# Three attentions of a four-block kernel: row maxima sent by DMA into the queries' tiles, remainders formed in pairs, the work of a round dealt anew

## The chip, the cores and the metric

The kernel runs on one core of a Trainium2 chip. The metric is the device time of one execution in microseconds; the time before is the median of three runs. Beside them stands one execution that was taken with the hardware profiler. All durations below come from that execution.

## The reference, cut to what matters

Four blocks follow each other on x of shape (4, 512, 288): an attention with a mixture of four experts, an attention with a dense layer, a rotation in a subspace, and another attention with a dense layer. All in float32. The change touches the three attentions (called 0, 1 and 3 after their blocks), each of 16 heads of 18 features:

```python
q, k, v = (h @ w_qkv + b_qkv) split into 16 heads of 18
attn = softmax(q @ k^T * 18 ** -0.5)          # per batch and head, 512 x 512
o = attn @ v
x = x + gate * (o @ w_proj + b_proj)
```

## The kernel before, in words

**Rounds and gaps.** An attention works off 16 rounds `r`, one for each batch `b` (4) and group `g` of four heads (4). A round has eight gaps `k` (`gaps = 2 * NT`). Each gap begins with a *quad* (`quad`): two row-max products (`row_max`, tiles a0m, a1m, a3m) for the present round, and two products for the weights (`weight`, tiles a0s, a1s, a3s) that lag ten gaps behind, so they belong to the round before or the one before that. The four products of a quad use 32 rows each (a head has 18 features, padded to 32), lie on the four row groups of TensorE, and run there together. Each fills one PSUM bank of 128x512. VectorE empties the banks of the row maxima (`tensor_reduce`, L1115), ScalarE those of the weights (`Exp`, L1127).

**What fills a gap after its quad.** `shift(r - 1)` in gap 0: the maxima stand in a tile `maxima` with one column for each head and query tile; four transposes on TensorE (tile a3sh and its like) bring them into rows, and VectorE subtracts them (L1170) from row 18 of each head's padded queries. The padded keys hold a one there, so the product for the weights already has the maximum taken off. `sums`: the weights of one key tile times the values (tile av, with a column of ones for the denominators); two key tiles in gap 2 and two in gap 6. `steps[k]`: layer norm, division, biases and loads. `pieces[k]`: a string of letters, each of which moves a job on by one step: Q (`queries_and_keys`, tiles psqk), X (`values`, tiles psv), P (`project`, tiles pp), A (`activations`, transposes), R (the experts' routing, in attention 0).

**Jobs.** A features' length of 288 is two chunks of 128 and a remainder of 32 (36 rows for `project`). A job's product is thus one remainder product and two whole chunks (four half-width ones for queries and keys). The remainder of tile or chunk `n` stands on row group `n % 4`; for `project` on one half of the array. Before, jobs take one tile after the other.

**Queries and keys on their way.** `queries_and_keys` leaves chunks of seven heads in an SBUF tile; DMAs from POOL's queue (L1055) spread each head's 18 rows to 32-row places in `pads`, which has `NR = 3` places for queries and three for keys. Before a place is used again POOL clears it (L193), and rows that came too early wait in `waiting`.

**Banks.** PSUM has eight banks of this size: four of tag "sc", three of tag "de", one for av. In the main loop of an attention (`wide`) each call of `bank` takes its tag from a ring:

```python
banks = {"sc": 4, "de": 3}
ring, turns, wide = ["sc"] * 4 + ["de"] * 2, [0], [False]
...
        if wide[0]:
            turns[0] += 1
            tag = ring[turns[0] % len(ring)]
```

Quads call `bank`, and so does `misc` (the transposes of `shift` and of `activations`, the routing). Jobs call `place`, which in the main loop takes a "de" bank by name, without the ring. A tile takes any free bank of its tag, and keeps it until it has been evicted.

**Order.** TensorE's products run in the order of the program (`mm` orders each behind the last). After the 16 rounds a last loop of five steps does the weights that lag, and then the hidden layer that follows begins. Attention 0 has other work beside it: `tick` moves a chain of reflections on VectorE and POOL (the subspace of the rotation), four times in a round, then twice; in attention 1 twice.

Of the kernel before, what the change touches and what calls it, by code (L numbers as in the profile page):

```python
# [25 lines left out]
NR = 3  # L26
# [22 lines left out]
def kernel(ctx: ExitStack, tc: tile.TileContext, a: dict, out: bass.AP):  # L49
# [128 lines left out]
    maxima = []  # L178
    for n in range(2):
        m = cst.tile([P, NT, NG * DP], F32, tag=f"max{n}", name=f"max{n}")  # L180
        nc.gpsimd.memset(m, 0.0)
        maxima.append(m)
    zeros = maxima[0].rearrange("p t c -> p (t c)")
# [4 lines left out]
    nc.vector.tensor_reduce(unit, ident[:, D::DP], AX.X, ALU.add)  # L188

    def cleared(engine, k):  # L190

        if k < NR:
            engine.memset(pads[:, k, :], 0.0)  # L193
        else:
            engine.tensor_copy(pads[:, k, :], unit.to_broadcast([P, T]))
# [95 lines left out]
    def attention_weights(l):  # L291
# [71 lines left out]
        def clear(engine, *some):  # L363
            return both(*[lambda k=k: cleared(engine, k) for k in some])

# [3 lines left out]
        order = (0, NR, 1, NR + 1, 2, NR + 2)  # L369
        if l == 0:  # L370
            late.append(clear(nc.gpsimd, *order))
        else:
            late += [clear(nc.vector, *order[0:3]), clear(nc.vector, *order[3:])]
# [171 lines left out]
    def warm(name, n):  # L545

        ps = bank("sc", name)
        for _ in range(n):
            mm(ps[:, 0 : T // 2], lhsT=ident, rhs=zeros[:, 0 : T // 2], start=True, stop=True)
            ordered(last[0], turned_rows[0])  # L550
# [450 lines left out]
    def attention(l, w, mod, eps, feed, ticks, hT=None, then=None, also=()):  # L1001
# [11 lines left out]
        with ExitStack() as es:  # L1013
            pool = es.enter_context(tc.tile_pool(name=name, bufs=2))
            hTs, xns, vs, raws, outs, gbs = {}, {}, {}, {}, {}, {}
            dens, ps, now = {}, {}, [0, True]
            waiting = []
# [5 lines left out]
            def place(what):  # L1023
                return misc(what) if now[1] else single("de", what)

            def values(b, *tiles):

                for t in tiles:
                    yield
                    if t == 0:  # L1030
                        vs[b] = pool.tile([P, NT, H, D + 1], F32, tag="v", name=f"{name}v{b}")
                        nc.gpsimd.memset(vs[b][:, :, :, D : D + 1], 1.0)
                    ps = place(f"{name}psv{b}_{t}")
                    for c in (MC, *range(MC)):
                        if c < MC:
                            yield
                        mm(
                            ps[:, 0:C],
                            lhsT=rows_of(hTs[b], c, t, slice(t * P, (t + 1) * P)),
                            rhs=rows_of(w["v"], c, t, slice(0, C)),  # L1040
                            start=(c == MC),
                            stop=(c == MC - 1),
                        )
                    o = vs[b][:, t, :, 0:D]
                    i = ps[:, 0:C].rearrange("p (h d) -> p h d", d=D)
                    if "bv" in w:
                        bv = w["bv"].rearrange("p (h d) -> p h d", d=D)
                        nc.vector.tensor_add(o, i, bv)
                    else:
                        nc.vector.tensor_copy(o, i)  # L1050

            def send(r, s, i, row, queue):

                to = pads[i * DP : i * DP + D, s * NR + r % NR, :]
                queue.dma_start(to, row)  # L1055

            def sent(r):

                for one in [one for one in waiting if one[0] == r]:
                    waiting.remove(one)  # L1060
                    send(*one, nc.gpsimd)

            def queries_and_keys(*some):

                for b, n in some:
                    yield
                    ps = place(f"{name}psqk{b}_{n}")
                    m = min(HC, 2 * H - n * HC) * D
                    rows, first = rest_of(n)
                    mm(  # L1070
                        ps[0:m, :],
                        lhsT=w["qkr"][rows, first : first + m],
                        rhs=hTs[b][rows, MC, :],
                        start=True,
                        stop=False,
                    )
                    for q in (slice(0, T // 2), slice(T // 2, T)):
                        for c in range(MC):
                            yield
                            mm(  # L1080
                                ps[0:m, q],
                                lhsT=w["qk"][:, c, n * HC * D : n * HC * D + m],
                                rhs=hTs[b][:, c, q],
                                start=False,
                                stop=(c == MC - 1 and q.stop == T),
                            )
                    t = pool.tile([HC * D, T], F32, tag="qk", name=f"{name}qk{b}_{n}", bufs=3)
                    nc.scalar.activation(  # L1088
                        t[0:m], ps[0:m], AF.Identity, bias=w["bqk"][0:m, n : n + 1]
                    )  # L1090
                    for g, s, i, k, at in heads_of(n):
                        for j in range(k):
                            row = t[(at + j) * D : (at + j + 1) * D, :]
                            one = (b * NG + g, s, i + j, row)
                            if one[0] < NR or one[0] <= now[0] + 1:
                                queue = nc.scalar if s and one[0] == 0 and n == 0 and i + j else nc.gpsimd
                                send(*one, queue)
                            else:
                                waiting.append(one)

            def heads_rows(i):
                return slice(i * DP, (i + 1) * DP)

            def row_max(r, t, i):

                m = maxima[r % 2].rearrange("p t (h d) -> p t h d", d=DP)
# [3 lines left out]
                    lhsT=pads[heads_rows(i), r % NR, t * P : (t + 1) * P],  # L1110
                    rhs=pads[heads_rows(i), NR + r % NR, :],
# [3 lines left out]
                take("DVE", nc.vector.tensor_reduce(m[:, t, i, D : D + 1], ps, AX.X, ALU.max))  # L1115

            def weight(r, t, i):
                ps = bank("sc", f"{name}s{r}_{t}_{i}")
                mm(
                    ps,  # L1120
                    lhsT=pads[heads_rows(i), NR + r % NR, t * P : (t + 1) * P],
                    rhs=pads[heads_rows(i), r % NR, :],
# [33 lines left out]
            def shift(r):  # L1156

                ps = misc(f"{name}sh{r}")
                m = maxima[r % 2]
                for t in range(NT):  # L1160
                    mm(
                        ps[:, t * P : (t + 1) * P],
                        lhsT=m[:, t, :],
                        rhs=ident,
                        is_transpose=True,
                        start=True,
                        stop=True,
                    )
                q = pads[:, r % NR, :]
                take("DVE", nc.vector.tensor_sub(q, q, ps))  # L1170
# [71 lines left out]
            def project(b, *groups):  # L1242
# [3 lines left out]
                for tiles in groups:  # L1246
                    yield
                    o = outs[b, "o"]
                    ps = [place(f"{name}pp{b}_{t}") for t in tiles]
# [29 lines left out]
            def others(r):  # L1279
# [7 lines left out]
                pieces = {1: "QQ", 3: "QQQ", 4: "PPP", 5: "PP", 7: "P"}  # L1287
                if b < 2:
                    pieces = {0: "Q", 1: "Q", 3: "Q", 4: "QQ"}
# [9 lines left out]
                if g < NG - 1 and b < B:  # L1299
                    jobs["Q"] = queries_and_keys((b, g + 2))  # L1300
                elif b + 1 < B:
                    jobs["Q"] = queries_and_keys((b + 1, 0), (b + 1, 1))
# [7 lines left out]
                if g == 1 and b + 1 < B:  # L1310
                    jobs["A"] = activations(b + 1)
                    jobs["X"] = values(b + 1, 0)
                    pieces = {0: "AA", 1: "QQ", 2: "A", 3: "QQQ", 4: "XXX", 5: "PP", 7: "P"}
                    if b < 2:
                        pieces.update({4: "X", 5: "X", 7: "X"})
                if g == 2 and b + 1 < B:
                    jobs["X"] = values(b + 1, 1, 2, 3)
                    pieces = {0: "XXX", 1: "QQ", 3: "QQQ", 4: "XXX", 5: "X", 7: "XX"}
                if g == 3 and b + 1 < B:
                    pieces = {0: "QQ", 1: "QQQ", 3: "QQ", 4: "QQQ", 5: "PP", 7: "P"}  # L1320
                    if b == 0:
                        pieces = {0: "QQ", 1: "QQQ", 3: "QQ", 4: "QQ", 5: "Q"}
                if r == n - 4:
                    pieces = {0: "PPP", 1: "QQ", 3: "QQQ", 4: "PPP", 5: "PP", 7: "P"}
                if r == n - 3:
                    pieces = {0: "Q", 1: "Q", 3: "Q", 4: "QQ"}
                if r == n - 2:
                    pieces = {0: "Q", 1: "Q", 3: "Q", 4: "QQ"}
                if r == n - 1:
                    pieces = {1: "PPP", 3: "PP", 4: "P", 5: "PP", 7: "P"}  # L1330


                if g == 2 and 0 < b < B:
                    for c in range(MC + 1):
                        steps[c].append(lambda c=c: divide(b - 1, c))
                if 0 <= r - 2 < n:
# [1346 lines left out]
```

## Time and profile before

| | us |
|---|---|
| median of 3 runs (lowest, highest) | 1905.28 (1903.22, 1907.09) |
| the profiled execution | 1910.58 |
| its span, first to last instruction | 1908.6 |
| TensorE busy in the span | 1852.5 (97%) |
| VectorE busy | 1069.1 (56%) |
| POOL busy | 743.9 (39%) |
| ScalarE busy | 720.8 (38%) |
| first to last quad, attentions 0, 1, 3 | 29 to 405, 862 to 1201, 1408 to 1742 |

Starts and durations are of the profiled execution, in us from its first instruction. TensorE's matmuls are pipelined and the ends of its rows are modelled; the time from the start of one item to the start of the next is what the item costs in the queue. One product in float32 gives two rows in the trace (two matmul instructions). PE is TensorE, PEld its weight loads, DVE VectorE, ACT ScalarE, POOL GpSimd, SP the engine whose queue starts most DMAs. In a row of the timeline stand the start, the length, the engine, the line, the operation, the written and read tiles, the shapes and the number of instructions that were merged; in brackets the idle time before it and what ended it.

### The profile page before, as it was taken

How to read it: one execution, taken by the hardware profiler on the slowest of the kernel's cores; microseconds unless marked ns; L12 is line 12 of the kernel's file. 1: busy time of each engine (PE TensorE's matmuls, PEld its weight loads, DVE VectorE, ACT ScalarE, POOL GpSimd, SP SyncE). 2: the span in 40 equal slices, each digit the busy share in tenths (PEclk: the TensorE clock that was granted, in tenths of full speed). 3: DMA queues.
4: the chain of work that ended last, by engine and by line, in shares of the span. 5: the costliest groups of instructions: out<-in, count | busy, mean ns of one | idle time of the engine just before them, and what ended most of it. 6: DMA issues, size and time to landing. Idle time of an engine off the chain costs nothing. (4 is left out here: it accounts for less than half of the span.)

```text
span 1908.6 us, 28581 instructions
## 1 busy us (share of the span) xinstructions
PE 1852.5 (97%) x10037; PEld 954.6 (50%) x10037; DVE 1069.1 (56%) x3171; ACT 720.8 (38%) x1347; POOL 743.9 (39%) x1204
## 2 busy tenths in 40 slices
PE   7999999998989998999999999999999999999998
PEld 4333333356767776774333333555643334334565
DVE  4767877725534555548767668252265666573201
ACT  1545545343222222223545455422125555455121
POOL 6253543434334346535734353222523344442101
PEclk9989999899989999999999999999999999999999
DMA  6442222326676666641312111300101221111000
GB/s 158 121 59 49 33 70 69 94 57 191 181 196 201 184 185 190 204 130 42 75 40 45 43 42 37 75 15 4 24 17 28 45 57 40 40 42 23 19 17 25
DMA packets 100547, 151.14 MB, mean 79 GB/s; under 512 B 42432, under 2 KB 77803, under 8 KB 100405
## 3 DMA queue, kind: packets, MB, share of 16 engines
q0 software_dynamic: 35280, 87.64, 16.5%
q1 hardware_dynamic: 64850, 61.45, 13.9%
q8 instruction: 80, 1.31, 0.3%
q14 instruction: 63, 0.51, 0.1%
q10 hardware_dynamic: 274, 0.23, 0.0%
HBM read 103.24 MB, written 20.08 MB: 65 GB/s over the span
## 5 line engine op out<-in xcount | busy, mean ns | idle before, releaser
L1115 DVE TENSOR_REDUCE max<-a3m 128x1 f32<-128x512 f32 x256 | 164.3, 684 | 103.6 <-PE a3s L89 100.0
L1115 DVE TENSOR_REDUCE max<-a1m 128x1 f32<-128x512 f32 x256 | 164.9, 683 | 72.0 <-PE a1s L89 68.8
L1115 DVE TENSOR_REDUCE max<-a0m 128x1 f32<-128x512 f32 x256 | 164.7, 682 | 62.1 <-PE a0s L89 59.4
L1127 ACT ACTIVATE a0p<-a0s 128x512 f32<-128x512 f32 x256 | 140.4, 596 | 155.3 <-PE a0s L89 143.7
L1127 ACT ACTIVATE a1p<-a1s 128x512 f32<-128x512 f32 x256 | 139.3, 596 | 138.0 <-PE a1s L89 132.9
L1127 ACT ACTIVATE a3p<-a3s 128x512 f32<-128x512 f32 x256 | 139.0, 596 | 133.1 <-PE a3s L89 129.7
L89 PE MATMUL e0h<-e0hT,e0w 128*128 128x256 f32 (+1 forms) x918 | 172.6, 400 | 5.4 <-ACT e0hT L2239 2.8
L89 PE MATMUL e0o<-e0w,e0hm 128*128 128x288 f32 x648 | 171.7, 415 | 3.1 <-DVE ef L966 3.1
L89 PE MATMUL a0m<-pads 32*128 32x512 f32 x512 | 165.6, 660 | 6.9 <-DVE max L1115 6.2
L89 PE MATMUL a0s<-pads 32*128 32x512 f32 x512 | 169.0, 673 | 1.6 <-ACT a0p L1127 1.4
L89 PE MATMUL a1s<-pads 32*128 32x512 f32 x512 | 159.8, 642 | 3.2 <-DVE max L1115 3.2
L89 PE MATMUL a1m<-pads 32*128 32x512 f32 x512 | 157.7, 640 | 0.3 <-DVE max L1115 0.2
L89 PE MATMUL a3s<-pads 32*128 32x512 f32 x512 | 156.4, 637 | 0.0
L89 PE MATMUL a3m<-pads 32*128 32x512 f32 x512 | 153.4, 636 | 1.1 <-DVE max L1115 1.1
L89 PEld LDWEIGHTS e0h<-e0hT,e0w 128*128 128x128 f32 (+1 forms) x918 | 131.3, 193 | 40.5 <-issue 17.4
L89 PEld LDWEIGHTS e0o<-e0w,e0hm 128*128 128x128 f32 x648 | 121.9, 193 | 36.0 <-DVE ef L966 3.9
L1588 ACT ACTIVATE e0hm<-e0h,e0w 128x256 f32<-128x256 f32 x144 | 60.3, 470 | 126.4 <-PE e0h L89 102.5
L2150 POOL DMA_INDIRECT e0w<-w1c,wrow x57 | 55.4, 971 | 123.3 <-PE e0h L89 66.7
L89 PEld LDWEIGHTS a0m<-pads 32*128 32x128 f32 x512 | 49.7, 189 | 69.5 <-DVE max L1115 33.2
L1055 POOL DMA_DIRECT2D pads<-a3qk x126 | 63.4, 509 | 52.8 <-ACT a3qk L1088 21.8
L89 PE MATMUL f1h<-f1hT,w 128*128 128x512 f32 (+1 forms) x216 | 81.2, 616 | 0.8 <-ACT f1hT L620 0.4
L1055 POOL DMA_DIRECT2D pads<-a0qk x126 | 64.0, 513 | 45.2 <-ACT a0qk L1088 14.8
(546 smaller groups left out, 3286.0 us busy)
## 6 DMA issues: line engine op xcount, KB each, us to landing
eo<-e0r SPq DMA_DIRECT2D x50, 144.0 KB
ada<-in_ada SPq DMA_DIRECT2D x18, 324.0 KB
wr<-in_wrot SPq DMA_DIRECT2D x16, 288.0 KB
xm<-e0m SPq DMA_DIRECT2D x6, 768.0 KB
pads<-a0qk POOLq DMA_DIRECT2D x126, 36.0 KB
pads<-a1qk POOLq DMA_DIRECT2D x126, 36.0 KB
pads<-a3qk POOLq DMA_DIRECT2D x126, 36.0 KB
g<-gates SPq DMA_DIRECT2D x24, 144.0 KB
```

The costliest lines, as they stand in the source:

```text
L89: ins = nc.tensor.matmul(*args, **kwargs).ins
L1055: queue.dma_start(to, row)
L1115: take("DVE", nc.vector.tensor_reduce(m[:, t, i, D : D + 1], ps, AX.X, ALU.max))
L1127: take("ACT", nc.scalar.activation(p, ps, AF.Exp, scale=D**-0.5))
L1588: nc.scalar.activation(self.hms[i][f], ps[r], func, bias=b1(f)),
L2150: gather = nc.gpsimd.indirect_dma_start(dst, None, table, bass.IndirectOffsetOnAxis(row, 0))
```

## The change

*Maxima.* They are written to a 128x32 tile, a column for each head and query tile. `shift(r)` comes at the end of round `r` (gap 7): VectorE transposes the tile in blocks of 32x32, and four DMAs from POOL's queue send the rows into row 18 of the padded queries. The padded keys hold minus one there, written once (`marked`). TensorE's transposes and VectorE's subtraction go. Row-max products use 18 rows of each head, products for the weights 19.

*Places and lag.* `NR` is 4, the clearing by POOL and the list `waiting` go, the weights lag twelve gaps (`LAG`), and the last loop has six steps. `sums` takes one key tile in each of gaps 0, 2, 4 and 6.

*Pairs.* `values`, `queries_and_keys` and `project` take two tiles or chunks at a time (some chunks of queries and keys stay single): first both remainders, then the chunks of the one and of the other. The first has a "de" bank, the second an "sc" bank.

*The deal.* `pieces` and `steps` are set anew; the experts' own setting for the last round goes.

```diff
-NR = 3
+NR = 4
+LAG = 12
...
+        m = cst.tile([P, DP], F32, tag=f"max{n}", name=f"max{n}")
...
+        rows_of_maxima.append(cst.tile([P, DP], F32, tag=f"mrow{n}", name=f"mrow{n}"))
...
+    nc.vector.tensor_scalar_mul(unit, unit, -1.0)
+    def marked(engine, k):
+        engine.tensor_copy(pads[:, NR + k, :], unit.to_broadcast([P, T]))
+    overwritten = 2 * (MC + 1) - NR
+    for k in range(overwritten, NR):
+        marked(nc.vector, k)
...
+            def place(what, k=0):
+                return misc(what) if now[0] else single(("de", "sc")[k], what)
...
+                    ps = [place(f"{name}psv{b}_{t}", k) for k, t in enumerate(tiles)]
...
+                    for k in range(len(tiles)):
+                        product(k, MC)
+                    for k, t in enumerate(tiles):
                         for c in range(MC):
                             yield
+                            product(k, c)
...
+            def queries_and_keys(b, *groups):
+                for ns in groups:
+                    yield
+                    ps = [place(f"{name}psqk{b}_{n}", k) for k, n in enumerate(ns)]
...
             def row_max(r, t, i):
+                rows = slice(i * DP, i * DP + D)
...
+                k = i * NT + t
+                to = maxima[r % 2][:, k : k + 1]
+                take("DVE", nc.vector.tensor_reduce(to, ps, AX.X, ALU.max))
             def weight(r, t, i):
+                rows = slice(i * DP, i * DP + D + 1)
...
             def shift(r):
-                for t in range(NT):
-                    mm(
-                        ps[:, t * P : (t + 1) * P],
-                        lhsT=m[:, t, :],
-                        rhs=ident,
-                        is_transpose=True,
...
-                q = pads[:, r % NR, :]
-                take("DVE", nc.vector.tensor_sub(q, q, ps))
+                m, t = maxima[r % 2], rows_of_maxima[r % 2]
+                take("DVE", nc.vector.transpose(t, m))
+                to = pads[D::DP, r % NR, :].rearrange("i (t k j) -> i t k j", k=P // DP, j=DP)
+                for k in range(P // DP):
+                    nc.gpsimd.dma_start(to[:, :, k, :], t[k * DP : k * DP + GH * NT, :])
...
-                pieces = {1: "QQ", 3: "QQQ", 4: "PPP", 5: "PP", 7: "P"}
+                pieces = {1: "QQ", 3: "QQQ", 5: "PP", 7: "PPP"}
                 if b < 2:
-                    pieces = {0: "Q", 1: "Q", 3: "Q", 4: "QQ"}
+                    pieces = {1: "QQ", 3: "QQ", 4: "Q"}
...
+                some = {0: [2], 1: [3, 4], 3: [0, 1]}
+                if b == B - 1:
+                    some = {0: [2], 1: [3], 2: [4]}
+                own = b + (g == NG - 1)
+                if own < B and g in some:
+                    jobs["Q"] = queries_and_keys(own, some[g])
...
                 if g == 1 and b + 1 < B:
                     jobs["A"] = activations(b + 1)
+                    pieces = {1: "QQ", 2: "A", 3: "QQQ", 4: "A", 5: "QQ", 6: "A", 7: "QQ"}
                 if g == 2 and b + 1 < B:
+                    jobs["X"] = values(b + 1, [0, 1], [2, 3])
+                    pieces = {1: "XXX", 3: "XX", 5: "XXX", 7: "XX"}
+                if g in (1, 2) and b == B - 1:
+                    pieces = {1: "QQ", 3: "QQ", 4: "Q"}
                 if g == 3 and b + 1 < B:
+                    pieces = {0: "QQ", 1: "QQQ", 2: "Q", 3: "QQQ", 5: "PP", 7: "PPP"}
+                if g == 3 and b == B - 1:
+                    pieces = {1: "P", 3: "PP", 5: "P", 7: "P"}
                 if g == 2 and 0 < b < B:
                     for c in range(MC + 1):
-                        steps[c].append(lambda c=c: divide(b - 1, c))
-                if 0 <= r - 2 < n:
-                    steps[5].append(lambda: invert(r - 2))
+                        steps[c + 2].append(lambda c=c: divide(b - 1, c))
+                if 0 <= r - 2 < n - 2:
+                    steps[7].append(lambda: invert(r - 2))
                 if g == 0 and b > 1:
+                    jobs["P"] = project(b - 2, [1, 3])
                 if g == 3 and b > 0:
+                    jobs["P"] = project(b - 1, [0, 2])
...
-                    quad([(row_max, r, k)] + lagging(8 * r + k - 10))
-                    if k == 0:
-                        shift(r - 1)
+                    quad([(row_max, r, k)] + lagging(gaps * r + k - LAG))
+                    if k == gaps - 1:
+                        shift(r)
                     for step in steps[k]:
                         step()
-                    if k == 2 and r > 1:
-                        sums(r - 2, 2)
-                        sums(r - 2, 3)
                     if k == 6:
                         sums(r - 1, 0)
-                        sums(r - 1, 1)
+                    elif k % 2 == 0 and r > 1:
+                        sums(r - 2, 1 + k // 2)
                     work_off(jobs, pieces.get(k, ""))
...
+            for k in range(LAG // 2):
+                u = gaps * n + 2 * k - LAG
+                quad(lagging(u) + lagging(u + 1))
```

## The prediction

> **What bounds the kernel now.** I read the page first: TensorE is busy for 1852.5 of 1908.6 us, VectorE for 56%. A busy TensorE can still be a waiting one, so I then asked for the busy time by stage, over the three attentions.
>
> ```profile
> 1408.00:1742.00 334.00, 331.27 (x1970) 128.21 (x1968) 214.89 (x412) 168.24 (x300) 128.61 (x235) 0.99 0.18 39
> 862.00:1201.00 339.00, 334.51 (x1969) 128.82 (x1962) 254.23 (x601) 168.85 (x300) 157.62 (x268) 0.99 0.20 46
> 29.00:405.00 376.00, 363.09 (x2108) 145.06 (x2106) 276.92 (x747) 171.31 (x307) 156.51 (x269) 0.95 0.33 75
> ```
>
> Columns: window, its length, busy time of PE, PEld, DVE, ACT, POOL, then granted clock and DMA. In all three TensorE (third column) fills the window; VectorE stands at 64 to 75%. So a round lasts as long as TensorE's queue of it, plus what that queue waits. The timeline of attention 3 shows the queue item by item; start to start is the price.
>
> ```profile
> 1550.08 0.69 PE L89 MATMUL a3m<-pads 32*128 32x512 f32 x1
> ...
> 1551.15 1.91 PE L89 MATMUL av<-a3p,a3v 128*19 128x512 f32 x16
> 1551.24 1.29 DVE L1115 TENSOR_REDUCE max<-a3m 128x1 f32<-128x512 f32 x2 [1.27 <-PE a3s L89]
> 1551.28 1.09 ACT L1127 ACTIVATE a3p<-a3s 128x512 f32<-128x512 f32 x2 [0.41 <-PE a3s L89]
> ...
> 1552.99 0.69 PE L89 MATMUL a3m<-pads 32*128 32x512 f32 x1
> ...
> 1553.98 1.02 PE L89 MATMUL a3psqk<-a3hT,wqkr 32*126 32x512 f32 x2
> ...
> 1554.92 0.70 PE L89 MATMUL a3psqk<-a3hT,wqk 128*126 128x256 f32 x2
> ...
> 1559.18 1.43 PE L89 MATMUL a3pp<-wp,a3oo 36*128 36x288 f32 x4
> ...
> 1560.55 0.69 PE L89 MATMUL a3m<-pads 32*128 32x512 f32 x1
> ...
> 1564.53 0.75 PE L89 MATMUL a3pp<-wp,a3oo 126*128 126x288 f32 x2
> ...
> 1565.21 0.69 PE L89 MATMUL a3m<-pads 32*128 32x512 f32 x1
> ...
> 1566.42 0.66 PE L89 MATMUL a3sh<-ident,max 128*128 128x128 f32 x4
> ...
> 1567.01 0.69 PE L89 MATMUL a3m<-pads 32*128 32x512 f32 x1
> ```
>
> A quad takes 1.07 us (1550.08 to 1551.15), two `sums` 1.84, the 32-row remainder of a queries-and-keys chunk 0.94 (1553.98 to 1554.92), a projected tile's remainder 0.68 (1559.18 to 1560.55 is 1.37, less 0.68 for whole chunks alone, 1564.53 to 1565.21), the four transposes of `shift` 0.59. VectorE and ScalarE empty a quad's banks 1.76 to 2.45 us after its start (1551.24 + 0.64 and + 1.29; ScalarE's two by 2.29). That matters where nothing stands between two quads:
>
> ```profile
> 1681.69 0.69 PE L89 MATMUL a3m<-pads 32*128 32x512 f32 x1
> ...
> 1683.54 1.12 PE L89 MATMUL a3s<-pads 32*128 32x512 f32 x2
> 1684.59 1.91 PE L89 MATMUL av<-a3p,a3v 128*19 128x512 f32 x16
> ```
>
> The second quad got two banks at once, out of the six that quads rotate through, and its last product had to wait until 1683.54, 1.85 us after the first quad's start. So a gap shorter than about 1.85 us is bound by the emptying of banks, and any longer one by TensorE. Nearly all are longer today.
>
> **The change, part by part, for one attention.**
>
> *Transposes of `shift` leave TensorE:* 16 x 0.59 = 9.4 us saved.
>
> *Remainders in pairs.* Two remainders on different row groups should run side by side. The experts' hidden layer already does this with four:
>
> ```profile
> L89 PE MATMUL e0h<-e0hT,e0w 32*128 32x256 f32 x306 | 26.5, 416 | 5.4 <-ACT e0hT L2239 2.8 <-issue 1.5 <-ACT a0p L1127 0.6
> ```
>
> 306 of 416 ns would be 127 us, yet they cover 26.5. Pairs made: 7 of queries and keys (four of chunks 0 and 1, three of 3 and 4; the last batch keeps 2, 3, 4 single), 8 of values, 6 of projections. 7 x 0.94 + 14 x 0.68 = 16.1 us saved. If they did not overlap, nothing would be.
>
> *Sums one by one:* half a pair costs
>
> ```profile
> 1736.43 1.05 PE L89 MATMUL av<-a3p,a3v 128*19 128x512 f32 x8
> ...
> 1737.42 2.00 PE L89 MATMUL a3s<-pads 32*128 32x512 f32 x8
> ```
>
> 0.99 instead of 0.92, so 0.14 more per pair, two pairs in each of 15 rounds: 4.2 us lost. *LAG 12:* two units of weights more have no row maxima beside them and make one more step at the end; such a step's quad took 1.93 us there (1737.42 to 1739.35): 1.9 lost. *New deal:* today the quad after the 0.68 us piece of gap 7 is stretched to 1.21 (1565.21 to 1566.42); 0.14 x 15 = 2.1 saved.
>
> *Bank tiles.* This decides. The second of a pair takes a bank of "sc" by name, from its remainder to its eviction, across gaps: with `pieces` as they are, in round g=1 it is held for quads 2 to 7 (6), in g=2 for 2, 3, 6, 7 (4), in g=3 for 1, 2, 3 (keys) and 6, 7 (projection), in g=0 from the third batch for 6, 7. By batches 13 + 15 + 17 + 8 = 53 of 128 quads. Then quads have 3 sc + 2 de = 5 banks. With one bank free at its start, a quad needs three of the last quad's four emptied, 2.29 us after that one's start and some 0.05 to be seen: 2.34. A gap with a single `sums` is 1.07 + 0.99 = 2.06, so it loses about 0.3; longer ones lose nothing. Worse: `bank` deals tags in a ring of four sc and two de. Quads that stand on even places get 4 sc, then 2 + 2, then 2 + 2; with three sc banks the fourth product of the 4-sc quad waits for the first of its own quad: 1.85 us, about 1.8 lost. On odd places quads get three sc and only the 0.3 to 0.45 of short gaps is lost. Today `shift` takes a place too, so a round moves the ring by 33 and the two kinds alternate; after, it moves by 32 and a kind stays for four rounds, until the three transposes of the next batch's activations flip it. I take half of the quads in each kind: 53/2 x 1/3 x 1.8 = 15.9; of the other 44, half stand behind a short gap: 22 x 0.3 = 6.6; and 2 for three-sc quads that wait for VectorE's last (2.5 instead of 2.34). Together 24.5 us. Bounds: all odd, 53 x 0.5 x 0.3 = 8; all even, 53/3 x 1.8 + 35 x 0.5 x 0.4 = 39.
>
> [...]
>
> *Off the path.* VectorE loses 16 subtractions of 0.68 and gains 16 transposes of 128x32, an instruction that the trace does not have: by the nearest rows between 0.17 (batch-norm aggregate) and 0.68. I take 0.2, as it is near the small ones in size; both ends are hidden. [...] POOL loses 13 memsets of 0.54 and gains 64 DMA issues of 0.51: 26 us more of some 129 to 157 busy in 330 or more. The new way of the maxima: the last two are reduced 2.45 after quad 7's start, + 0.2 transpose + 4 x 0.51 issue + one DMA from issue to use, 2.07 (a3one at 1560.74, its reader on SP at 1562.81): 6.8 us. The first reader is the weights of gap 4 of the next round, 2.7 + 2.1 + 2.6 + 2.1 + 2.5 = 12 us after that start: about 5 us of cover. These DMAs pass POOL's queue behind `collect`'s of gap 4 and the keys' of gap 3, both done by then; behind them wait the gated adds of gap 7, which nobody hurries for. Products with 18 or 19 rows for 32: nothing, as 128-row ones of 512 columns (604 ns mean) take no longer than 32-row ones (about 640). `divide` two gaps later and `invert` in gap 7: VectorE's pieces of 0.24 to 0.8 us, beside TensorE's queue as before; where VectorE is late its evictions are late, and in attentions 0 and 1, where it is busy for 74 to 75%, a held bank costs more than reckoned; I leave that to the upper bound.
>
> **The sum.** 9.4 + 16.1 + 2.1 - 4.2 - 1.9 = 21.5 saved, 24.5 lost: 3 us more per attention, 9 in all. The profiled execution took 1910.58 (1908.6 of span and 2.0 around), 5.3 over the median; the difference is carried to the median: 1905.28 + 9 = 1914. Bounds: 3 x (8 - 21.5) = -40 gives 1865, 3 x (39 - 21.5) = +53 gives 1958.
>
> **The rivals.**
> 1. *TensorE's savings win: faster.* The place is the same 53 quads, and the point that decides is a price of 21.5/53 = 0.41 us for each: below it the change gains. If most batches fall on odd places, or the free bank is nearly always there, the losses go to 8 to 20 and the time to 1865 to 1901. For it: TensorE is the bound and 25.5 us of its work per attention truly goes. Against it: the 1.85 us wait is in the trace with six banks, and here there are five. At prices between 0.38 and 0.43 it comes out as no change.
> 2. *The maxima come late.* If POOL or the DMA needs over 5 us more than reckoned, every round waits; 2 us late in 47 rounds gives 94 more, some 2008. Against it: POOL is idle for more than half of each round.
> 3. *The pairs do not run side by side,* so that this part doesn't do what it says: 3 x 16.1 = 48 more, 1962. Against it: the experts' row above.
>
> **How the numbers follow.** Forecast (banks cost more than the pairs save, slower): 0.60. Cancelled within 0.2%, which is about what a measurement of this kernel can tell from no change (3.8 us): 0.09. Rival 1: 0.25. Rival 2: 0.04, rival 3: 0.02. Slower: 0.60 + 0.04 + 0.02 = 0.66. The range 1880 to 1946 leaves out the far ends of rival 1 (about 0.1) and of the banks with rivals 2 and 3 (about 0.1). The forecast's own range is 1909 to 1946.
>
> **What would show it.** Right: no a0sh, a1sh or a3sh; TensorE's waits in a?m and a?s for max (26 to 33 us per attention on PEld today, in the list of waits) grow; some quads last about 2.8 us from first product to next item, two or so in every second batch's g=1 round, so that these rounds take 23 to 25 us where others take 19. Attentions 1 and 3 differ, as one begins on even places where the other begins on odd. Right on the cover: no weights wait for a DMA. Wrong: quads in rounds with pairs at 1.07 throughout and rounds of 18 to 20 us (rival 1), PE waiting for DMA at gap 4 (rival 2), two psqk remainders 0.9 us apart (rival 3).

## The result, and the profile after

The changed kernel takes 2102.76 us (median of 4 runs, 2070.38 to 2110.92) where the kernel before, on the same chip, takes 1904.25 (1902.35 to 1907.09). Three of the five executions of the changed kernel are over 1.5% longer than its fastest and count as slow, so every comparison below goes by the two others, 2070.38 and 2086.64 us, or 2078.5 in the middle. That is 174 us over the kernel before, a ratio of 1.0914 with a 95% interval of 1.0837 to 1.0991. The direction of the forecast holds; the size, 9 us of forecast against 174 measured, does not, and the time lies far outside the range of 1880 to 1946.

The profiled execution took 2070.38 us, its span is 2068.6. First the page of the kernel after, busy times and the row of the granted clock in 40 slices; the last line is the clock row of the kernel before:

```profile
PE 1994.4 (96%) x9845; PEld 968.0 (47%) x9845; DVE 1051.9 (51%) x3166; ACT 721.5 (35%) x1347; POOL 834.3 (40%) x1353
...
PEclk8799989679999999979778997999975999997999
...
PEclk9989999899989999999999999999999999999999
```

TensorE executes fewer instructions than before (9845 for 10037) and is busy for 142 us more (1994.4 for 1852.5). Work went and time came, so the same instructions take longer. The clock rows say why: slices at 5, 6 and 7 tenths, where before none lies under 8. The windows of the three attentions (columns as in the prediction: window, length, busy PE, PEld, DVE, ACT, POOL, clock, DMA) say where:

```profile
26.00:447.00 421.00, 402.23 (x2042) 147.94 (x2042) 272.53 (x747) 170.38 (x307) 189.61 (x324) 0.84 0.30 68
895.00:1295.00 400.00, 392.00 (x1905) 136.63 (x1905) 249.28 (x600) 169.52 (x300) 188.28 (x321) 0.83 0.17 38
1504.00:1897.00 393.00, 382.81 (x1904) 133.78 (x1904) 210.10 (x412) 168.41 (x299) 161.29 (x289) 0.84 0.15 34
```

The clock is 0.84, 0.83 and 0.84, where it was 0.95, 0.99 and 0.99. The attentions are 45, 61 and 59 us longer; the rest of the kernel changed by a few us. TensorE is busy all the time, as before. Three stretches of attention 3 of the kernel after, the first two at half clock, the last at full clock:

```profile
1522.00:1542.50 20.50, 20.19 (x63) 7.86 (x62) 7.42 (x12) 6.72 (x10) 4.81 (x10) 0.50 0.06 14
1545.90:1610.80 64.90, 63.36 (x192) 20.87 (x190) 17.63 (x30) 15.78 (x28) 15.88 (x28) 0.50 0.07 14
1659.00:1805.00 146.00, 143.31 (x854) 52.22 (x850) 88.93 (x165) 73.16 (x131) 73.79 (x133) 1.00 0.20 43
```

The clock records of these two executions (24 before, 60 after) have two values only, 1 and 0.5, and the half-clock stretches last 3.41 us or a multiple of it, up to 64.9 (the last one after, 9.3, is cut off by the end). Before there are 12 of them in the kernel, 75 us together, 6.3 us each on average; after there are 30, 429 us together, 14.3 us each. Half of the half-clock time, the most that it can cost, is 38 us before and 215 after. The difference of 177 covers the 160 us by which the profiled spans differ. One quad and one `sums` in the half-clock stretch, and the same at full clock (timeline, TensorE):

```profile
1598.17 1.21 PE L90 MATMUL a3m<-pads 18*128 18x512 f32 x1
...
1600.19 1.92 PE L90 MATMUL av<-a3p,a3v 128*19 128x512 f32 x8
...
1602.04 1.22 PE L90 MATMUL a3psqk<-a3hT,wqk 128*126 128x256 f32 x2
```

```profile
1701.11 0.69 PE L90 MATMUL a3m<-pads 18*128 18x512 f32 x1
...
1702.18 1.05 PE L90 MATMUL av<-a3p,a3v 128*19 128x512 f32 x8
...
1703.16 0.69 PE L90 MATMUL a3m<-pads 18*128 18x512 f32 x1
...
1704.12 1.02 PE L90 MATMUL a3psqk<-a3hT,wqkr 32*126 32x512 f32 x2
1705.07 0.70 PE L90 MATMUL a3psqk<-a3hT,wqk 128*126 128x256 f32 x2
```

The quad takes 2.02 us (1598.17 to 1600.19) in place of 1.07, the `sums` 1.85 in place of 0.98. At full clock everything costs what the prediction said.

**Theories.** A: the clock follows how many rows of the array are fed; 18 and 19 rows in place of 32 lower it, though the rows left out held only zeros. B: the waits for held banks lower it. C: fewer TensorE instructions lower it. Each run below also tests my sum at a fixed clock, +9 us: with the cause of the low clock undone, the time should come back to about that.

### The profile page after: what moved, and what is told of

It reads as the page before. It is cut to its first block, busy times and chain, and to the rows that moved or that the text cites. A ratio compares the mean times of both kernels' runs of the same rounds, so it can differ in the third digit from the quotient of the medians.

```text
span 2068.6 us, 28504 instructions
## 1 busy us (share of the span) xinstructions
PE 1994.4 (96%) x9845; PEld 968.0 (47%) x9845; DVE 1051.9 (51%) x3166; ACT 721.5 (35%) x1347; POOL 834.3 (40%) x1353
## 5 line engine op out<-in xcount | busy, mean ns | idle before, releaser
L90 PE MATMUL a0s<-pads 19*128 19x512 f32 x512 | 188.8, 714 | 10.8 <-DVE max L1107 5.7
L90 PE MATMUL a3s<-pads 19*128 19x512 f32 x512 | 186.9, 730 | 7.7 <-DVE max L1107 7.7
L90 PE MATMUL a1s<-pads 19*128 19x512 f32 x512 | 186.9, 730 | 4.6 <-DVE max L1107 3.8
L90 PE MATMUL a1m<-pads 18*128 18x512 f32 x512 | 183.0, 754 | 6.4 <-DMA pads<-a1qk 4.3
L90 PE MATMUL a0m<-pads 18*128 18x512 f32 x512 | 182.2, 732 | 7.0 <-DVE max L1107 2.9
L1155 POOL DMA_DIRECT2D pads<-mrow x192 | 112.1, 590 | 167.7 <-DVE a3den L1196 49.8
L90 PE MATMUL a3m<-pads 18*128 18x512 f32 x512 | 171.9, 723 | 2.0 <-DVE max L1107 1.3
L90 PEld LDWEIGHTS a1m<-pads 18*128 18x128 f32 x512 | 51.7, 214 | 89.1 <-issue 37.1
L90 PEld LDWEIGHTS a0m<-pads 18*128 18x128 f32 x512 | 52.7, 210 | 81.8 <-issue 35.5
L90 PEld LDWEIGHTS a3m<-pads 18*128 18x128 f32 x512 | 49.0, 205 | 79.5 <-issue 39.9
```

Of the source, the lines that this page charges most:

```text
L90: ins = nc.tensor.matmul(*args, **kwargs).ins
L1155: nc.gpsimd.dma_start(to[:, :, k, :], t[k * DP : k * DP + GH * NT, :])
```

## The experiments

Each comparison is with the kernel before on the same chip, of four runs or more (of two for the kernel after). "Half" is the half-clock time in the profiled execution, with the number of stretches.

| kernel | median, us | ratio to before (95%) | clock | half, us |
|---|---|---|---|---|
| before | 1904 to 1911 | 1 | 0.981 | 75 in 12 |
| after | 2078.5 | 1.0914 (1.0837, 1.0991) | 0.897 | 429 in 30 |
| before, 18 and 19 rows | 1934.49 | 1.0142 (1.0101, 1.0184) | 0.966 | 134 in 19 |
| before, 18 rows in maxima alone | 1916.81 | 1.0050 (1.0022, 1.0078) | 0.976 | 95 in 17 |
| after, 32 rows in weights alone | 1993.01 | 1.0457 (1.0399, 1.0515) | 0.946 | 218 in 28 |
| after, 32 rows | 1973.43 | 1.0316 (1.0284, 1.0348) | 0.964 | 145 in 24 |
| after, ring of five | 1971.73 | 1.0347 (1.0293, 1.0401) | 0.935 | 255 in 16 |
| 32 rows, ring of five | 1927.20 | 1.0109 (1.0064, 1.0154) | 0.961 | 151 in 18 |
| 32 rows, singles | 1927.07 | 1.0096 (1.0064, 1.0129) | 0.969 | 122 in 19 |
| 32 rows, ring of five, LAG 10 | 1986.36 | 1.0403 (1.0366, 1.0439) | 0.949 | 205 in 27 |
| 32 rows, singles, LAG 10 | 1998.93 | 1.0479 (1.0446, 1.0512) | 0.949 | 205 in 26 |
| 32 rows, ring by need, LAG 10 | 1991.84 | 1.0437 (1.0403, 1.0470) | 0.953 | 187 in 26 |
| 32 rows, ring of five, maxima by SP | 1925.48 | 1.0109 (1.0080, 1.0139) | 0.965 | 136 in 20 |
| 32 rows, ring of five, LAG 10, by SP | 1949.31 | 1.0219 (1.0192, 1.0247) | 0.958 | 165 in 21 |
| 32 rows, ring of five, fillers | 1948.96 | 1.0227 (1.0191, 1.0262) | 0.967 | 130 in 13 |

### Rows: on the kernel before, and on the kernel after

The rows alone, in the kernel before:

```diff
-                    lhsT=pads[heads_rows(i), r % NR, t * P : (t + 1) * P],
-                    rhs=pads[heads_rows(i), NR + r % NR, :],
+                    lhsT=pads[slice(i * DP, i * DP + D), r % NR, t * P : (t + 1) * P],
+                    rhs=pads[slice(i * DP, i * DP + D), NR + r % NR, :],
...
-                    lhsT=pads[heads_rows(i), NR + r % NR, t * P : (t + 1) * P],
-                    rhs=pads[heads_rows(i), r % NR, :],
+                    lhsT=pads[slice(i * DP, i * DP + D + 1), NR + r % NR, t * P : (t + 1) * P],
+                    rhs=pads[slice(i * DP, i * DP + D + 1), r % NR, :],
```

> The kernel before, with one edit: products of row maxima read 18 and those of weights 19 of the 32 rows of a head (the rows left out hold zeros, nothing of the computation is lost). Theory A (TensorE's clock follows how many rows of the array are fed, so the 18 and 19 rows of the change lower it): the granted clock falls from 0.98 to about 0.90, the half-clock time grows from 75 to over 300 us, and the time goes to 2050 to 2110 us. Theory B (waits for held banks lower the clock) and theory C (fewer TensorE instructions lower it): no bank and no instruction changes here, so 1900 to 1912 us and a clock of 0.98.

> The kernel before, with 18 of 32 rows in the products of row maxima alone, the weights keep 32. Theory A: half of the loss of the run with both, so 1940 to 2020 us; if the clock has a threshold, it may be anything from 1905 to 2060. Theory B and theory C: no change, 1900 to 1912 us.

Measured 1934.49 and 1916.81 us. The first is 1.4% slower than before, with no bank, no wait and no instruction changed, and the data the same: theory A is shown in its direction, and B and C cannot make this difference. But it is 24 us and not the 140 to 200 that theory A alone expected. The second is a small part of it, 6 us. The clock of the two kernels in their profiled executions, before and with 18 and 19 rows:

```profile
core 0: 1908.6 us, clock 0.981
...
core 0: 1928.8 us, clock 0.966
```

In the kernel after, the rows are put back:

```diff
+        late.append(both(*[lambda k=k: marks.memset(pads[:, k, :], 0.0) for k in range(NR)]))
...
-                rows = slice(i * DP, i * DP + D)
+                rows = slice(i * DP, (i + 1) * DP)
...
-                rows = slice(i * DP, i * DP + D + 1)
+                rows = slice(i * DP, (i + 1) * DP)
...
+                if NR <= r + 1 < n:
+                    steps[1].append(lambda: unshifted(r + 1))
...
+            def unshifted(r):
+                zeros = pads[D + 1 :: DP, 2 * NR - 1, :]
+                nc.sync.dma_start(pads[D::DP, r % NR, :], zeros)
```

> The kernel after, with 32 rows in both kinds of product again. The rows above the 18th must then hold zeros while maxima are formed, so one more DMA on SP in each round sets row 18 of the queries to zero and four memsets per attention clear their places. Theory A: the clock is back at 0.97 to 0.98, and the time is what the sum without clock said, 1890 to 1925 us. Theory B and theory C: banks and instruction counts are those of after, so the clock stays at about 0.90 and the time at 2050 to 2120 us.

> The kernel after, with 32 rows in the products of weights alone; the row maxima keep 18. Theory A: half of the quads' products are full again, so the clock lies between, 0.92 to 0.97, and the time between 1930 and 2040 us. Theory B and theory C: no change, 2060 to 2115 us.

Measured 1973.43 and 1993.01 us. The same rows are worth 105 us here, over four times as much as in the kernel before, and half of them (the weights alone) already some 85. Yet 1973 is not the 1890 to 1925 of theory A, and the clock stays at 0.964. So the rows act together with something else in the change.

### Banks: the ring, and singles

```diff
-    ring, turns, wide = ["sc"] * 4 + ["de"] * 2, [0], [False]
+    ring, turns, wide = ["sc"] * 3 + ["de"] * 2, [0], [False]
```

> The run with full rows (1973 us), with one more edit: quads take their banks in a ring of three sc and two de instead of four and two, so that no quad asks for four sc while the second of a pair holds one. Theory A with my bank term (quads that ask for a held bank cost 1.8 us each): the 35 quads of about 2.8 us in the three attentions fall to about 15, which gives back 36 us, and with fewer waits some half-clock time goes too: 1905 to 1940 us. Rival (the waits come from the emptying of banks by VectorE and ScalarE, whatever the tags): five banks in the ring are no better than six, 1965 to 2000 us.

> The kernel after, with its 18 and 19 rows, with the ring of three sc and two de alone. If rows alone set the clock: the half-clock time stays over 350 us and only the bank waits go, 2030 to 2065 us. If rows and waits set it together: the half-clock time falls to 150 to 250 us, and the time to 1950 to 2010 us. Rival (the tags don't matter): 2065 to 2110 us.

Measured 1927.20 (46 us less) and 1971.73 (107 us less), both in the ranges that a joint effect was expected to give; the half-clock time of the second, 255 us, is a little over. The one line of the ring is worth 107 us where the products have 18 and 19 rows and 46 where they have 32. If the rows alone or the waits alone set the clock, it would be worth about the same in both. The two act together: with both undone 1927, with the rows alone at fault 1972, with the ring alone 1973, with both 2078.5, which is 61 us more than the two added up.

The mean quad in full-clock stretches of attention 3 lasts 1.17 us before, 1.41 with full rows, 1.24 with the ring of five as well (116, 123 and 122 quads of which all eight records are in the trace); those of 2.8 us and more number 0, 12 and 0. TensorE's own waits for the eviction of maxima in the second product of that attention, with full rows and with the ring of five as well (total us, times, longest):

```profile
PE a3s L90 <- DVE max L1108: 8.7, 10, 1.7
...
PE a3s L90 <- DVE max L1108: 4.2, 1, 4.2
```

One such wait in the trace of the kernel after:

```profile
1639.08 1.02 PE L90 MATMUL a3psqk<-a3hT,wqkr 32*72 32x512 f32 x4
1640.04 0.70 PE L90 MATMUL a3psqk<-a3hT,wqk 128*126 128x256 f32 x2
1640.66 0.69 PE L90 MATMUL a3m<-pads 18*128 18x512 f32 x1
...
1642.57 1.12 PE L90 MATMUL a3s<-pads 19*128 19x512 f32 x2 [0.77 <-DVE max L1107]
1643.62 1.05 PE L90 MATMUL av<-a3p,a3v 128*19 128x512 f32 x8
```

The pair's two remainders cost 0.96 us (1639.08 to 1640.04), no more than a single one (0.95, at 1704.12 above): the pairs do run side by side. The quad behind them lasts 2.96 us, as its last product waits for a bank until 1642.57. That is 1.9 us over a quad of 1.07 and fits the four-sc quad of the prediction, which was to lose about 1.8; the trace does not name the tag of a bank.

Singles, with full rows: the second tile of a pair has no sc bank any more, each remainder stands alone (`values(b + 1, [0], [1], [2], [3])` and its like, `pieces` one letter longer where a job has one step more).

> The run with full rows (1973 us), with remainders one by one and every piece in a de bank, as before the change; transposes by VectorE, the DMAs, LAG 12 and single sums stay. Theory A with my bank term: no sc bank is held, the mean quad goes from 1.50 to about 1.25 us (33 us less per attention), the remainders cost 16 us more per attention, and half-clock time falls by some 40 us: 1895 to 1930 us. Rival (pairs pay for their banks): the 48 us of remainders come on top, 2000 to 2025 us.

Measured 1927.07 us, as the first expectation had it, and the same as pairs with the ring of five. So with the kernel's own ring a pair costs in waits more than its remainder saves: 1973 for 1927. With the ring of five it gains back nothing over singles.

### The way of the maxima

What is left is 1% over before. LAG 10 shortens the thin ends of an attention, where the weights that lag have no row maxima beside them:

```diff
-LAG = 12
+LAG = 10
...
-                    if k == 6:
-                        sums(r - 1, 0)
+                    if k in (4, 6):
+                        sums(r - 1, k // 2 - 2)
                     elif k % 2 == 0 and r > 1:
-                        sums(r - 2, 1 + k // 2)
+                        sums(r - 2, 2 + k // 2)
...
```

> Full rows and the ring of five (1927 us), with LAG 10 again, so that the weights follow two gaps sooner, rounds 1 have two quads fewer without a partner, and the end of an attention one step less. By the reading of the traces so far (a 3.4 us stretch in which TensorE streams under some 440 columns per us, counted by rows over 128 and column groups over 4, is followed by half clock), the thin ends of the attentions shrink: 3 x (3 to 5) us of steps and 20 to 40 us of half-clock time less, 1895 to 1915 us. Rival (the maxima now come late, as their way of 6.8 us has only some 7 us of cover): PE waits for DMA at gap 2 in every round, 1 to 2 us in 47 rounds, 1970 to 2020 us.

> Full rows and singles (1927 us), with LAG 10 again: what is left of the change is the maxima's way by VectorE and DMA, the single sums and the new deal. Same reading: 1890 to 1915 us; by my terms the transposes alone would give 28 us less than before, so below 1905 if the clock comes back to 0.98. Rival (maxima late): 1970 to 2020 us.

> As the run with the ring of five and LAG 10, but quads use the ring of five only while the second of a pair holds an sc bank, and the ring of six otherwise. If a sixth bank still matters where no pair is held: 5 to 15 us below the run with the ring of five; if not, the same within 5 us.

Measured 1986.36, 1998.93 and 1991.84 us: misses of mine, 59 to 72 us slower than with LAG 12. The first two lie in the range of the rival, late maxima, though these come not in every round. The list of waits of the first:

```profile
PE a1s L90 <- DMA pads<-mrow: 24.3, 5, 7.2
PE a3s L90 <- DMA pads<-mrow: 17.5, 4, 5.7
PE a0s L90 <- DMA pads<-mrow: 10.0, 3, 5.4
```

The maxima are late in 12 places, mostly in the rounds that begin a batch, by up to 7.2 us: in attention 3 these rounds last 26.7, 26.7 and 26.3 us in place of 22.2, 20.2 and 20.1, and each of the three has 6.8 us of half clock behind its wait. So rival 2 of the prediction is real two gaps further on; LAG 12 is what holds it off. The run with the ring by need shows nothing of a sixth bank beside this, and that question stays open.

The next two send the maxima from SP's queue (`nc.sync` for `nc.gpsimd` in `shift`):

> Full rows and the ring of five at LAG 12 (1927 us), with the 192 DMAs of the maxima issued by SP instead of POOL. PE waited for these DMAs for 10 us in all there. If POOL's queue is what delays them, these waits go and POOL is free 112 us more: 1910 to 1925 us. If SP's own queue of broadcasts and loads delays them as much: 1920 to 1960 us.

> The run with LAG 10 (1986 us), with the maxima's DMAs issued by SP. There PE waited 5 to 7 us in the rounds that begin a batch (rounds of 26 to 28 us where others take 19 to 21), and POOL's queue also holds the gated bias and the keys in these rounds. If POOL's queue is the cause: these rounds come down to 20 to 22 us and the time to 1900 to 1930 us. If the way is too long in itself: 1970 us or more.

Measured 1925.48 and 1949.31 us. At LAG 12 the queue makes no difference (1927.20 with POOL). At LAG 10, SP gives 37 us back, so POOL's queue was a good part of the lateness, but not all: 1949 lies between the two expectations.

### Work for the clock

```diff
+            def more(u):
+                mm(bank("sc", f"{name}w{u}"), lhsT=ident, rhs=w["qk"][:, 0, 0:T], start=True, stop=True)
...
+                    if gaps * r + k < LAG:
+                        more(k)
...
                 quad(lagging(u) + lagging(u + 1))
+                more(gaps + k)
```

> Full rows and the ring of five at LAG 12 (1927 us), with one product of 128 rows and 512 columns, read by nobody, after each of the four quads of round 1 that have no weights beside them, and after each of the six steps at the end of an attention: 30 in all, 0.43 to 0.9 us each. By the reading that the streamed work of a 3.4 us stretch decides (threshold about 440 columns per us), each adds 512 columns twice where a stretch has 0.2 to 0.35 of the full rate: the half-clock time falls from 151 to 90 to 120 us, and the time, with the fillers' own 13 us, to 1910 to 1927 us. By the reading that only TensorE's idle time counts (it is busy for 95% and more in these stretches already), the half-clock time stays and the fillers cost their time: 1935 to 1950 us.

Measured 1948.96 us, slower by 22 than without fillers; half-clock time fell from 151 to 130 us only. Neither expectation holds as a whole: the time lies in the range of the second, which had the half-clock time unchanged. In round 1 they did what they were to do: the half-clock stretches there (13.7, 6.8 and 6.8 us) are gone, and the three rounds take 23.4, 21.8 and 21.5 us in place of 25.7, 22.3 and 22.1. At the ends of the attentions they take a place in the ring and wait for ScalarE, as the weights' products there do (in the kernel after, their weight loads wait for it 4.5 us, 7 times, in the last 37 us of attention 3):

```profile
PE a0w L90 <- ACT a0p L1121: 3.7, 6, 0.7
PE a3w L90 <- ACT a3p L1121: 3.3, 5, 0.7
PE a1w L90 <- ACT a1p L1121: 3.3, 5, 0.7
```

The ends (last maximum to last weights) grew from 25.7, 19.8 and 21.3 us to 35.4, 26.3 and 26.3, 21 us together, where the three rounds had gained 3.4.

No version of the changed kernel beats the kernel before; the nearest, 1925.48 and 1927, lie 1% above it.

## Why the prediction was wrong

**The step that failed** is the half sentence "Products with 18 or 19 rows for 32: nothing". Its reason, that a product of fewer rows takes as long as one of more, is true of one product at a given clock (1.07 us a quad with 32 rows before, 1.07 with 18 and 19 at 1701.11). It left out that the clock is not given. The whole sum took the 0.95, 0.99 and 0.99 of the windows before as fixed. In the kernel after, putting the rows back is worth 105 of the 174 us.

The rows are not all: with them put back the time, 1973, is still outside the range. The pairs were forecast to cost 25 us net (73.5 of banks, less 48.3 of remainders, in three attentions); 1973.43 for 1927.07 says 46. All the other terms were to save 16 us (5.4 in each attention); 1927.07 against 1908.48 for the kernel before on that chip says 19 lost. The three together, 105, 46 and 19, make 170 of the 174 us; the kernel before itself differs by up to 7 us from chip to chip. Each is a price beside the parts that were still in place, as the rows and the ring act together.

**How rows and waits multiply.** What follows is a count of my own, made from the matmul and clock records of these traces and fitted to them. It takes each 3.41 us stretch of the grid on which the recorded clock changes, and in it for each matmul record its columns, times its rows over 128, times its output columns, rounded up to 32, over 128 (a record of 18*128 18x512 counts 512 x 18/128 = 72, one of 128*19 128x512 counts 512 x 32/128 = 128). Over the traces of before and after, a stretch with under 444 such columns per us is followed by half clock and one with more by full clock, in 1130 of 1138 stretches (444 is the value that parts these two traces best); in the 13 other traces, of which six were taken after it was formed, in 7211 of 7261. Each part of the count is there because the records of before and after ask for it: without the share of rows it is wrong 124 times in place of 8, without the share of output columns 50 times, each with the value that suits it best. Most stretches only go on as they were, so the changes are the better test: before and after together the clock falls 41 times and comes back 40 times, and the count has 40 of these falls and 38 of these returns. This is a reading of the records; the fillers of round 1 are the one trial of it that was made on purpose. That rows and held banks act together is shown by the runs; that this count is what joins them is argued from the reading. By it:

| | columns | at full clock, per us | at half clock, per us |
|---|---|---|---|
| quad, 32 rows (8 records of 128) | 1024 | in 1.07 us: 957 | in 2.02 us: 507 |
| quad, 18 and 19 rows (72 and 76) | 592 | 553 | 293 |
| one `sums` (8 records of 128) | 1024 | in 0.98 us: 1045 | in 1.85 us: 554 |

At full clock both kinds of quad lie over 444. But by this reading, once a wait has brought half clock, quads of 32 rows still stream 507 and end it, and quads of 18 and 19 stream 293 and keep it: the kernel is held at half clock by its own slowness until a dense piece of the queue comes. That fits the counts: held banks make the falls more frequent (19 and 18 with singles or ring of five, 24 with held banks, all with full rows), few rows make each last longer (8.4 us on average with 32 rows and the ring of five, 15.9 with 18 and 19). The kernel before has few waits (10 of TensorE's own for the eviction of maxima, 11.7 us together, where the kernel after has 32, 24.4 us), so its rows matter little (24 us); the change brought both.

A rival reading is that the clock goes by how long TensorE is busy. It agrees with the falls: the stretches of the kernel after that turn from full to half clock have a median busy share of 0.77. It does not agree with the returns: of the 106 half-clock stretches that were followed by another in the kernels before and after, 88 were busy for over 95%, such as the 63.36 of 64.90 us above. The busy time that the profile shows does not tell when the clock returns: over the 751 half-clock stretches of all 15 traces no value of it does better than to guess half clock each time (301 wrong), where the columns are wrong 29 times; in before and after alone these are 40 and 4 of 146.

**Point by point.** 
- Transposes of `shift`: gone, no a?sh in the trace. VectorE's transpose takes 211 ns, as taken (0.2).
- Pairs: side by side, as forecast; rival 3 is out.
- Sums one by one: 0.98 us, as taken (0.99).
- Banks: right in kind, somewhat small in size. The mean quad grew by 0.24 us with full rows, 31 us for 128 quads where the forecast had 24.5. The quads of 2.8 us and more are 12 in attention 3, where half of 53, a third of them, had given 9. And its worst effect, the falls of the clock, was not in it.
- Maxima: the cover of some 5 us at gap 4 holds, as PE waits for these DMAs in three places only, 6.7 us together; two gaps earlier it fails. Four issues on POOL take 2.3 us (582 ns each, median, where I took 510):

```profile
PE a0s L90 <- DMA pads<-mrow: 4.5, 1, 4.5
PE a0m L90 <- DMA pads<-mrow: 1.4, 1, 1.4
PE a1s L90 <- DMA pads<-mrow: 0.8, 1, 0.8
...
L1155 POOL DMA_DIRECT2D pads<-mrow x192: 567/582/677, 52.4 to 1877.0; - x192
L1152 DVE STREAM_TRANSPOSE mrow<-max x48: 195/211/213, 51.9 to 1874.7; 128x32 f32<-128x32 f32 x48
```

- The sum without the clock: taking half of the half-clock time off the spans, after with full rows is 1971.3 - 72.3 = 1899 and before 1908.6 - 37.5 = 1871, 28 us more where the forecast had 9 and its bounds were -40 and +53. It is inside the bounds, but rough, as waits shrink at half clock (the quad takes 2.02 us there for 1.07, while VectorE's reductions of maxima take 0.69 us, median, in the stretches from 1545.9 at half clock and from 1659.0 at full clock alike); it shows the sum and not its terms, which may be off and make up for each other.
- Rival 1, that the savings win, is out as well: even with full rows and no bank held in vain the kernel is 1% slower than before. Of these 19 us, LAG's longer ends are a part (from the last maximum to the last weights an attention takes 25.7, 19.8 and 21.3 us with the ring of five, and 21.1, 15.9 and 16.0 before); the rest was not taken apart. Theory C, fewer TensorE instructions, has no run of its own and may have a share in it.

The prediction listed "what would make it wrong" only within full clock: long quads, late DMAs, remainders apart. A look at the row of the granted clock in the windows, and at what the change does to the work per stretch, was missing.

## What to carry to other kernels

Price an edit on TensorE twice: in time at the clock that is granted, and in the work that a stretch of some microseconds still holds, since in the traces of before and after the clock of the next stretch went with it (1130 of 1138). Trimming rows that hold zeros saved no time on TensorE here (a quad took 1.07 us at full clock either way) and took work out of the count (592 for 1024 a quad); with the lighter quads and the held banks the kernel stood at half clock for 429 us, with 32 rows and the same banks for 145. And when a wait is added to a queue that is already light, read the granted clock of that stage first: here the rows alone cost 24 us, the rest of the change alone 63, and both together 174.

## What was not expected of the hardware

Leaving out rows of zeros lowered the clock: the kernel before with the same products on the same data, but without 14 and 13 zero rows of each head, ran 1.4% slower, at a mean clock of 0.958 to 0.966 in four runs where 13 runs of the kernel before have 0.977 to 0.983. TensorE was busy for 63.36 of 64.90 us (98%) in the kernel after, at a granted clock of 0.50 throughout. And the count above is sensitive to the 19 output columns of `sums`: in the traces of before and after it is wrong 8 times with them taken as 32, and 38 times with the true 19, at the value that suits it best. Rounding up to 16, which also makes 32 of 19, does as well (8), rounding up to 64 does not (38); no run tried this on purpose.
